# Attending: one PSUM bank for all key tiles in turns of four matmuls, and a longer rest in the gating

## The chip, the cores and the metric

The kernel runs on one core of one Trainium2 chip. The metric is the device time of one execution in microseconds (us). The kernel before takes 6137.45 us in the median of three runs (6137.38 to 6148.23).

## The reference

Input is x, 8 batches of 128 channels on a 36 x 36 grid, so 1296 tokens of 128 numbers per batch, all in float32. Cut to what matters:

```python
x = x + L0_conv_ref(group_norm(x), ...)         # convolutional attention block
t = tokens(x)                                   # (8, 1296, 128)
t = t + L1_attn_ref(layer_norm(t), ...)         # additive attention
t = t + L1_ffn_ref(layer_norm(t), ...)          # experts that choose their tokens

def L1_attn_ref(x, mask, Wq, bq, Wk, bk, w, bw):
    q, k = x @ Wq.T + bq, x @ Wk.T + bk
    scores = (tanh(q[:, :, None] + k[:, None]) * w).sum(-1) + bw
    return softmax(scores) @ x

def L1_ffn_ref(x, gate_w, gate_b, weight1, weight2):
    probs = softmax(x @ gate_w.T + gate_b, axis=tokens)   # 64 experts
    # each expert takes its 8 best tokens, pools them, runs two layers with a gelu,
    # and adds its output, weighted, to these tokens
```

The additive attention needs a tanh for every pair of tokens and every channel. Its scores are the bulk of the kernel's time.

## The kernel before

**Scores.** The kernel gets the scores from products of exponentials: for each pair of tokens it sums terms, and a term is a numerator divided by a denominator, where both are matmuls of a key feature (kf) with a query feature (qf). Queries of a batch are worked in three chunks of 432 (CH), keys in eleven tiles: ten of 128 and a last one of 16, which is put sixth (the list `order`, 0 to 4, 10, 5 to 9). One chunk and one key tile make a unit. A full unit has twelve slots, numbered k = 0 to 11, the small one has two. In all there are 2928 slots, and the loop of lines 1113 to 1146 writes out the program slot by slot.

In each slot, TensorE makes two numerators n and, for the slot three ahead (LAG), two denominators d (line 949). Each contracts 32 rows in two of three slots and 64 rows in the third. ScalarE takes the logarithm of d (line 972), and every second slot the exponential of its negative (line 975), which gives lq = 1/d. VectorE multiplies n by lq (line 1003), and GpSimd adds up the products (lines 1010 and 1012). In slots 2, 5, 8 and 11 (DVE_PAIRS) VectorE does the adding too (lines 992 to 999), so it has four operations there (three in slot 2) and not two.

**Banks.** The numerators and all side work share a pool of four PSUM banks, ps_n (line 151). A slot needs two of them for its n. `aux` takes one of the same four. The denominators have two double banks of their own.

**Side work.** All else of the layers is written as Python generators and taken up between the slots. They stand in four lanes, in this order of rank: first_of_all, urgent (the attending, and the first key features), gates (the gating) and background (the next batch's first layer, its tokens and key features). A generator yields what it wants next: `matmuls(rest)`, a turn on TensorE after so many slots, or `step(rest)`, a turn on the other engines. `TAKE` is a step in the next slot. `take_turns` (line 1072) runs the steps at the start of a slot, but not in DVE_PAIRS except for the first lane. `matmul_turn` (line 1077) runs one turn with matmuls at the end of a slot. Turns are paced: each turn's columns are counted (`bmm` adds the columns of its output, at least 128, and 20 more), every slot earns 400 (PACE), and a lane other than the first waits while the balance is below zero or the next slot is one of DVE_PAIRS. The gates lane also waits while urgent has work.

**Attending.** When the eleven exponentials e of a chunk are there (line 1032), `attend` (line 747) is put in the urgent lane. It works through the chunk's four query tiles of 108 tokens. For each, TensorE multiplies e by the normalized tokens xh, which carry a column of ones, so that the sum of the weights comes along: eleven products of 108 x 129 (function `weigh`). The product of the 16-token key tile uses xr, a copy of those tokens on the rows on which its e lies, and contracts 16 rows. The eleven are made in two turns of 6 and 5, each into a bank of its own. The first bank is copied to the tile `sums` (line 770), the second is added to it in the bank (line 772), and then VectorE closes the query tile: reciprocal (774), scaling and residual (775) and the statistics for the next normalization (779 and 780). For the last chunk of all, `attend_early` (line 724) sums nine key tiles while the scores of the last two are still being made.

**Gating.** `gate_logits` (line 793) follows for a whole batch. It computes the inverse root of the variances on GpSimd (`rsqrt`, into rs), and then for each chunk transposes the tokens (tp2), copies them (t2T), stores them, transposes them back in pairs (tp3), and scales each pair by rs (line 830). Between the copy and the first tp3 it asks for a rest of one slot (line 822). For the last batch it is called for one chunk at a time, from `attend`.

The order on every engine is the order of the written program. Semaphores between the engines are set by the framework.

Of the kernel before, what the change touches and what calls it, by code (L numbers as in the profile page):

```python
# [10 lines left out]
F32 = mybir.dt.float32  # L11
# [4 lines left out]
NB, C, H, W = 8, 128, 36, 36  # L16
# [7 lines left out]
T = 108  # L24
# [3 lines left out]
NKT = len(KT)  # L28
# [42 lines left out]
def kernel(  # L71
# [28 lines left out]
    nc = tc.nc  # L100
# [29 lines left out]
    with ExitStack() as loop, ExitStack() as score:  # L130
# [9 lines left out]
        chunks = pool("chunks", 8)  # L140
# [18 lines left out]
        def aux(name):  # L159
            return ps_n.tile([128, 512], F32, tag="n", name=name)  # L160
# [116 lines left out]
        def matmuls(rest=0):  # L277
            return (True, rest)
# [441 lines left out]
        def attend_early(b, c, es):  # L720

            xh, _, xr = prepared[b]
            held = [chunk_tile("sums") for _ in range(TPC // 2)]
            for i in range(TPC):
                at = (i % 2) * (C + 1)
                sums = early[i] = held[i // 2][:T, at : at + C + 1]
                for some in (order[:5], order[6 : NKT - 2] + order[5:6]):
                    pa = aux("pa1")[:T, : C + 1]
                    weigh(pa, i, some, es, xh, xr)
                    yield TAKE  # L730
                    if some[0] == order[0]:
                        nc.vector.tensor_copy(sums, pa)
                    else:
                        nc.vector.tensor_add(sums, pa, sums)
                    yield matmuls()

        def weigh(pa, i, some, es, xh, xr):

            for j in some:
                if j < NKT - 1:  # L740
                    e, v = es[j][:, i * T : (i + 1) * T], xh[:, j, :]
                else:
                    rows = slice(32 * i, 32 * i + REM)
                    e, v = es[j][rows, :T], xr[rows]
                bmm(pa, e, v, start=(j == some[0]), stop=(j == some[-1]))

        def attend(b, c, es):


            xh, _, xr = prepared[b]  # L750
            if c == 0:
                t2 = big_tile("t2").rearrange("p (t c) -> p t c", c=128)
                mv = two.tile([T, NT, 2], F32, tag="t2_mv", name="t2_mv")
                attended[b] = (t2, mv)
            t2, mv = attended[b]
            own = range(c * TPC, (c + 1) * TPC)
            for at in own:
                nc.sync.dma_start(t2[:T, at, :], tokd[b][at * T : (at + 1) * T])
            for i, at in enumerate(own):
                if i in early:  # L760
                    parts, sums = (order[NKT - 2 :],), early[i]
                else:
                    parts = (range(6), range(6, NKT))
                    sums = two.tile([T, C + 1], F32, tag="sums", name="sums")
                for some in parts:
                    pa = aux("pa1")[:T, : C + 1]
                    weigh(pa, i, some, es, xh, xr)
                    yield TAKE
                    if some[0] == 0:
                        nc.vector.tensor_copy(sums, pa)  # L770
                        yield matmuls()
                nc.vector.tensor_add(pa, pa, sums)
                inv = small.tile([T, 1], F32, tag="inv", name="inv")
                nc.vector.reciprocal(inv, pa[:, C : C + 1])
                nc.vector.scalar_tensor_tensor(
                    t2[:T, at, :], pa[:, :C], inv, t2[:T, at, :], ALU.mult, ALU.add
                )
                st = small.tile([T, 6], F32, tag="t2_st", name="t2_st")
                nc.vector.bn_stats(st, t2[:T, at, :])
                nc.vector.bn_aggr(mv[:, at, :], st)  # L780
                yield matmuls()
            if c == NCH - 1:
                prepared.pop(b)
            if b == NB - 1:
                yield from gate_logits(b, [c])
# [7 lines left out]
        def gate_logits(b, chunks):  # L793
# [23 lines left out]
            for c in chunks:  # L817
                tp, tt = turned(c, "t2T")
                yield TAKE
                nc.vector.tensor_copy(tt, tp[:, :CH])  # L820
                nc.sync.dma_start(t2d[b][:, c * CH : (c + 1) * CH], tt)
                yield matmuls(1)
                for j0 in range(0, TPC, 2):
                    tp = aux("tp3")
                    for j in (j0, j0 + 1):
                        turned_to(tp[:T, j * C : (j + 1) * C], tt[:, j * T : (j + 1) * T], ident)
                    yield TAKE
                    for j in (j0, j0 + 1):
                        t = c * TPC + j
                        nc.vector.tensor_scalar(  # L830
                            t2[:T, t, :], tp[:T, j * C : (j + 1) * C],
                            mv[:, t, 0:1], rs[:, t - tiles[0] : t - tiles[0] + 1],
                            ALU.subtract, ALU.mult,
                        )
                    yield matmuls()
# [522 lines left out]
```

The softmax here doesn't subtract the row's maximum and nothing guards it: scores larger than these inputs give would overflow.

## Time and profile before

| What | Value |
|---|---|
| Runs, median (lowest to highest) | 6137.45 us (6137.38 to 6148.23) |
| Profiled execution, its own time | 6140.74 us |
| Span of its instructions | 6139.0 us |
| Mean granted TensorE clock | 0.985 |
| TensorE busy / weight loads | 5957.9 us (97%) / 2862.1 us (47%) |
| ScalarE busy | 5279.9 us (86%) |
| VectorE busy | 4796.4 us (78%) |
| GpSimd busy | 4597.7 us (75%) |
| Attending's products of full key tiles (pa from xh and e) | 1920 records, 0.273 us in the median |
| Attending's products of the 16-token tile (pa from xr and e) | 192 records, 0.312 us in the median |
| Line 770, copy of the first sums | 92, 26.6 us busy |
| Line 772, addition of the two sums | 96, 28.0 us busy |

Times in the profile are microseconds unless marked ns. PE is TensorE, PEld its weight loads, DVE is VectorE, ACT ScalarE, POOL GpSimd, SP the engine that issues most DMAs. L949 is line 949 of the kernel. A float32 matmul leaves two records. An arrow in brackets names what ended the idle time of an engine before a row. The ends of matmuls are modelled and matmuls overlap, so that a busy TensorE is not one at its peak. A window is counted in us from the span's start.

### The profile page before, as it was taken

The numbers are of one execution on the slowest core, as the hardware profiler recorded it, in microseconds if no ns is written. First come the engines' busy times: TensorE is split into PE (matmuls) and PEld (weight loads), VectorE is DVE, ScalarE is ACT, GpSimd is POOL, SyncE is SP. The second block draws the span as 40 slices with busy tenths as digits, with TensorE's granted clock in tenths as the row PEclk, the third lists the DMA queues.
The fourth block names the chain that finished last, engine by engine and source line by source line (L and its number), as shares of the span: only waits on it lengthen the run. The fifth ranks groups of instructions, "written<-read, shape, count | busy, mean of one in ns | idle before, by whom it ended". The sixth has DMA issues, their size and how long they took to land.

```text
span 6139.0 us, 93072 instructions
## 1 busy us (share of the span) xinstructions
PE 5957.9 (97%) x33480; PEld 2862.1 (47%) x33480; DVE 4796.4 (78%) x9521; ACT 5279.9 (86%) x5371; POOL 4597.7 (75%) x2819
## 2 busy tenths in 40 slices
PE   7999999999999999999999999999999999999996
PEld 5454444544544445444455444454444544544443
DVE  4787878877788787877888777887778877788882
ACT  1888898888988888889998889888898888999990
POOL 4777777777787777778778786877777777787870
PEclk9999999999999999999999999999999999999997
DMA  1210011100110002100111001110011100110008
GB/s 44 70 37 22 25 62 38 34 25 28 68 43 20 26 27 71 39 24 23 44 55 39 22 24 59 44 39 22 20 65 40 34 25 28 58 50 29 28 20 297
DMA packets 151519, 270.87 MB, mean 44 GB/s; under 512 B 45648, under 2 KB 76752, under 8 KB 151056
## 3 DMA queue, kind: packets, MB, share of 16 engines
q1 hardware_dynamic: 151056, 264.92, 13.0%
q8 instruction: 264, 4.33, 0.3%
q14 instruction: 199, 1.63, 0.1%
HBM read 200.41 MB, written 64.19 MB: 43 GB/s over the span
## 4 chain that ended last, share of the span: by engine, by line
PE 77%; ACT 7%; DVE 6%; issue 6%; POOL 2%; DMA 1%; SPq 0%; DVEq 0%; POOLq 0%; ACTq 0%
PE n L949 37%; PE d L949 12%; PE pa L284 7%; PE pc L284 5%; ACT lq L972 5%; PE s L284 3%; PE pk L284 3%; PE pq L284 3%; DVE rp L1003 2%; DVE n L997 1%; DVE accd L999 1%; PE d L954 1%; ACT lq L975 1%; DMA w<-in_weight_dram 1%; PE n L954 1%
## 5 line engine op out<-in xcount | busy, mean ns | idle before, releaser
L1012 POOL TENSOR_TENSOR accp<-accp,rp 128x864 f32<-128x864 f32 x1440 | 2915.8, 2025 | 1041.0 <-DVE rp L1003 948.8
L949 PE MATMUL n<-qf,kf 32*128 32x432 f32 (+1 forms) x11520 | 3325.3, 574 | 46.5 <-ACT e L1032 13.3
L949 PE MATMUL d<-qf,kf 32*128 32x432 f32 (+1 forms) x11520 | 2991.6, 561 | 38.7 <-ACT lq L972 38.2
L972 ACT ACTIVATE lq<-d 128x864 f32<-128x864 f32 x2928 | 2524.2, 878 | 542.6 <-PE d L949 512.1
L1003 DVE TENSOR_TENSOR rp<-n,lq 128x432 f32<-128x432 f32 x3912 | 2173.3, 600 | 743.5 <-PE d L949 542.8
L975 ACT ACTIVATE lq<-lq 128x1728 f32<-128x1728 f32 (+1 forms) x1464 | 2398.2, 1638 | 46.3
L949 PEld LDWEIGHTS n<-qf,kf 32*128 32x128 f32 (+1 forms) x11520 | 1206.4, 184 | 1600.3 <-DVE rp L1003 581.5
L949 PEld LDWEIGHTS d<-qf,kf 32*128 32x128 f32 (+1 forms) x11520 | 1090.0, 185 | 422.1 <-issue 224.7
L997 DVE TENSOR_TENSOR n<-n,lq 128x432 f32<-128x432 f32 x1440 | 814.9, 608 | 142.1 <-PE n L949 88.5
L999 DVE TENSOR_TENSOR accd<-n,accd 128x432 f32<-128x432 f32 x1440 | 866.3, 602 | 24.6
L1010 POOL TENSOR_TENSOR accp<-rp 128x864 f32<-128x864 f32 x240 | 485.2, 2022 | 197.7 <-DVE rp L1003 195.6
L711 POOL TENSOR_SCALAR qf<-qf,cs_s 128x432 f32<-128x432 f32 x192 | 260.9, 1365 | 45.0 <-ACT qf L710 44.4
L284 PEld LDWEIGHTS pa<-xh,e 128*108 128x108 f32 x1920 | 222.5, 174 | 131.1 <-DVE rp L1003 56.0
L1021 POOL TENSOR_TENSOR accd<-accp,accd 128x432 f32<-128x432 f32 x240 | 265.2, 1105 | 18.8
L1019 POOL TENSOR_TENSOR accp<-accp 128x432 f32<-128x432 f32 x240 | 264.4, 1102 | 16.7
L284 PE MATMUL pa<-xh,e 128*108 128x129 f32 x1920 | 262.9, 283 | 8.7 <-ACT e L1032 5.2
L284 PE MATMUL s<-q,k 128*116 128x432 f32 x480 | 230.3, 568 | 1.7 <-DVE q L316 1.4
L284 PEld LDWEIGHTS pk<-xT,a_k 128*128 128x128 f32 x1408 | 171.2, 192 | 107.0 <-DVE n L997 33.7
L462 POOL TENSOR_TENSOR tot<-tot,e 116x432 f32<-116x432 f32 x192 | 212.0, 1104 | 6.0 <-ACT e L471 4.6
L471 ACT ACTIVATE e<-s 116x432 f32<-116x432 f32 x240 | 124.9, 520 | 98.3 <-PE s L284 97.9
L284 PE MATMUL pa<-e,vw 116*128 116x432 f32 x480 | 204.6, 549 | 0.0
L284 PE MATMUL pk<-xT,a_k 128*128 128x128 f32 (+1 forms) x1408 | 202.5, 287 | 0.1
(213 smaller groups left out, 3788.4 us busy)
## 6 DMA issues: line engine op xcount, KB each, us to landing
kf<-kd SPq DMA_DIRECT2D x239, 512.0 KB
kd<-ks SPq DMA_DIRECT2D x158, 256.0 KB
w<-in_weight_dram SPq DMA_DIRECT2D x32, 1024.0 KB
wk_t<-wk_t_d SPq DMA_DIRECT2D x7, 768.0 KB
wv_t<-wv_t_d SPq DMA_DIRECT2D x7, 768.0 KB
wq_t<-wq_t_d SPq DMA_DIRECT2D x7, 768.0 KB
x<-in_x_dram SPq DMA_DIRECT2D x8, 648.0 KB
t<-tokd SPq DMA_DIRECT2D x96, 54.0 KB
```

Source lines behind the costliest of these rows:

```text
L284: mm(out, lhsT, rhs, **kw)
L711: nc.gpsimd.tensor_scalar(qf[:, 1, :], qf[:, 0, :], cs_s[:, q : q + 1], None, ALU.mult)
L949: mm(outs[h][:, :CH], kf[rows[h], q, :], qf_of[b, c, q][rows[h], part, :], start=True, stop=True)
L972: nc.scalar.activation(lq[:, o : o + n, :], d[:, :n, :CH], AF.Ln)
L975: nc.scalar.activation(some, some, AF.Exp, scale=-1.0)
L997: mult(ns[h], ns[h], lq[:, o + h, :])
L999: nc.vector.tensor_add(live["d"], ns[h], live["d"])
L1003: mult(rp[:, h, :], n, lq[:, o + h, :])
L1010: nc.gpsimd.tensor_add(live["p"], live["r"], rp)
L1012: nc.gpsimd.tensor_add(live["p"], live["p"], rp)
L1019: nc.gpsimd.tensor_add(s[:, 0, :], s[:, 0, :], s[:, 1, :])
L1021: nc.gpsimd.tensor_add(d, s[:, 0, :], d)
```

## The change

Three things change.

The eleven products of a query tile all go into one bank, in the order of `order`, and `weigh` becomes a generator: it gives up its turn after every fourth product. So a query tile takes three turns, of 4, 4 and 3 products, and the product of the 16-token tile is the sixth. The copy to `sums` and the addition fall away, except for the four query tiles of the last chunk, whose early sums are added as before.

In `attend_early` the nine products of a query tile go into one bank in turns of 4, 4 and 1. One addition per query tile falls away.

In `gate_logits` the first chunk asks for a rest of four slots, not one, between the copy of t2T and the first tp3, except in the last batch.

```diff
         def attend_early(b, c, es):
...
                 sums = early[i] = held[i // 2][:T, at : at + C + 1]
-                for some in (order[:5], order[6 : NKT - 2] + order[5:6]):
-                    pa = aux("pa1")[:T, : C + 1]
-                    weigh(pa, i, some, es, xh, xr)
-                    yield TAKE
-                    if some[0] == order[0]:
-                        nc.vector.tensor_copy(sums, pa)
-                    else:
-                        nc.vector.tensor_add(sums, pa, sums)
-                    yield matmuls()
+                pa = aux("pa1")[:T, : C + 1]
+                yield from weigh(pa, i, order[: NKT - 2], es, xh, xr)
+                nc.vector.tensor_copy(sums, pa)
+                yield matmuls()
 
         def weigh(pa, i, some, es, xh, xr):
-            for j in some:
+            for x, j in enumerate(some):
                 if j < NKT - 1:
                     e, v = es[j][:, i * T : (i + 1) * T], xh[:, j, :]
                 else:
                     rows = slice(32 * i, 32 * i + REM)
                     e, v = es[j][rows, :T], xr[rows]
-                bmm(pa, e, v, start=(j == some[0]), stop=(j == some[-1]))
+                last = x == len(some) - 1
+                bmm(pa, e, v, start=(x == 0), stop=last)
+                if last:
+                    yield TAKE
+                elif x % 4 == 3:
+                    yield matmuls()
 
         def attend(b, c, es):
...
             for i, at in enumerate(own):
+                pa = aux("pa1")[:T, : C + 1]
+                yield from weigh(pa, i, order[NKT - 2 :] if i in early else order, es, xh, xr)
                 if i in early:
-                    parts, sums = (order[NKT - 2 :],), early[i]
-                else:
-                    parts = (range(6), range(6, NKT))
-                    sums = two.tile([T, C + 1], F32, tag="sums", name="sums")
-                for some in parts:
-                    pa = aux("pa1")[:T, : C + 1]
-                    weigh(pa, i, some, es, xh, xr)
-                    yield TAKE
-                    if some[0] == 0:
-                        nc.vector.tensor_copy(sums, pa)
-                        yield matmuls()
-                nc.vector.tensor_add(pa, pa, sums)
+                    nc.vector.tensor_add(pa, pa, early[i])
                 inv = small.tile([T, 1], F32, tag="inv", name="inv")
...
         def gate_logits(b, chunks):
...
                 nc.sync.dma_start(t2d[b][:, c * CH : (c + 1) * CH], tt)
-                yield matmuls(1)
+                yield matmuls(1 if c > chunks[0] or b == NB - 1 else 4)
```

## The prediction

> **What bounds the kernel now.** I began with the page: its engine shares and the chain that ended last.
>
> ```profile
> span 6139.0 us, 93072 instructions
> ...
> PE 5957.9 (97%) x33480; PEld 2862.1 (47%) x33480; DVE 4796.4 (78%) x9521; ACT 5279.9 (86%) x5371; POOL 4597.7 (75%) x2819
> ...
> PE 77%; ACT 7%; DVE 6%; issue 6%; POOL 2%; DMA 1%; SPq 0%; DVEq 0%; POOLq 0%; ACTq 0%
> ```
>
> TensorE (PE) carries 77% of the chain, but that is an average over stages. So I took two stretches of the last batch, where no other background work stands: one without side work, and one that is the attending of one chunk (slots 6 to 23 after it became due).
>
> ```profile
> core 0: us, PE busy (x) PEld busy (x) DVE busy (x) ACT busy (x) POOL busy (x), PEclk, DMA share, GB/s
> 5516.00:5549.00 33.00, 32.24 (x156) 12.69 (x154) 25.45 (x47) 32.61 (x36) 30.02 (x18) 1.00 0.05 17
> 5564.90:5600.50 35.60, 35.48 (x234) 20.52 (x232) 31.23 (x74) 30.08 (x30) 24.41 (x14) 1.00 0.08 26
> ```
>
> Without side work ScalarE (ACT) is busy 32.61 of 33 us and sets the pace. While attending it idles 5.5 us of 35.60: there TensorE and VectorE (DVE) hand the path to each other, as the timeline of the first attended query tile shows.
>
> ```profile
> 5564.41 1.58 PE L284 MATMUL pa<-xh,e 128*108 128x129 f32 x12 [0.54 <-DVE accd L999]
> 5564.91 1.11 DVE L1003 TENSOR_TENSOR rp<-n,lq 128x432 f32<-128x432 f32 x2
> ...
> 5565.92 0.63 PE L949 MATMUL n<-qf,kf 32*128 32x432 f32 x2
> ...
> 5566.86 0.99 PE L949 MATMUL n<-qf,kf 64*128 64x432 f32 x4
> 5567.02 1.12 DVE L1003 TENSOR_TENSOR rp<-n,lq 128x432 f32<-128x432 f32 x2 [0.69 <-PE d L949]
> ...
> 5568.06 1.12 DVE L997 TENSOR_TENSOR n<-n,lq 128x432 f32<-128x432 f32 x2
> 5568.51 1.13 PE L284 MATMUL pa<-xh,e 128*108 128x129 f32 x8
> 5569.57 0.36 PE L284 MATMUL pa<-xr,e 16*108 16x129 f32 x1
> ...
> 5570.24 0.29 DVE L772 TENSOR_TENSOR pa<-pa,sums 108x129 f32<-108x129 f32 x1
> ...
> 5571.58 1.10 DVE L1003 TENSOR_TENSOR rp<-n,lq 128x432 f32<-128x432 f32 x2
> ```
>
> Read from it: a turn of six products (12 records, two per product) holds TensorE 5565.92-5564.41 = 1.51 us; eight full records up to the 16-row ones take 1.06. So 0.11 per record and 0.19 per turn: 1.07 for four products, 0.85 for three. A slot of 32-row products takes TensorE 5566.86-5565.92 = 0.94, one of 64-row products 5568.51-5566.86 = 1.65. Products reach VectorE 5567.02-5565.92 = 1.10 after they begin. Slot 8 is VectorE's: 3.52 us from 5568.06 to 5571.58, 2.26 of its own four operations and 1.26 of the query tile's closing (lines 772 to 780). Slot 7 was TensorE's: VectorE idled 0.69.
>
> The gating's wait is in the answer on its scale column t_rs, here as it stands for the whole kernel:
>
> ```profile
>   POOL t_rs L265: 6.6, 7
> ```
>
> That is 0.94 us each in seven batches.
>
> **What the skill says.** The Trainium skill, "TensorEngine Tiling (Array Packing)", Key Properties: changing the tiling mode drains TensorE. The trace agrees in part: weights for a full-array turn are loaded only after 0.62 us of idle behind row-tiled products, and each turn costs its fixed 0.19. "TensorE: Matmul & The Clock Gate", The mechanism: a weight load overlaps running products only if its rows differ. Here the 16-row products at 5569.57 overlap the next slot's (n also begins at 5569.58), so at the end of a turn they cost nothing. "Perfetto Trace Analysis", Optimization Strategy: repeated equal gaps can mean too little PSUM for the next tile; the trace has TensorE's weight loads for n waiting 581.5 us on VectorE's line 1003 over the kernel.
>
> **The change, part by part.** The build of the changed kernel (not run) gives the order and PSUM banks of both programs. In both, 23 of 24 attendings lie in the loop. Before, each has eight turns of 6 and 5 products, 16 of them in slots 6, 8, 9, 11, 14, 15, 17, 20. After, all 23 have twelve, of 4, 4, 3, in slots 6, 8, 9, 11, 12, 14, 15, 17, 18, 20, 21, 23.
>
> Removed: 92 copies (0.289 us each, line 770), 92 of the 96 additions of line 772 (0.292; the four early query tiles keep theirs) and the early part's four (line 734, 0.285): 188 operations, 26.6+26.9+1.1 = 54.6 us of VectorE. The copies overlap TensorE's next products; only the addition of 0.30, in the closing, lies on the path where VectorE has it: the closing falls from 1.26 to 0.95.
>
> Added on TensorE, per query tile: one turn, 0.19; and the 16-row product, formerly last, now sixth, amid full ones. Its switch into row mode was shared with the turn's end; now it stands alone, and so does one back. The trace does not show it inside a turn. Lower bound 0 if loads hide it, upper 0.4 (two whole fixed turn costs); I take 0.20, one switch more.
>
> Added waits: one of four banks (ps_n) stays with the query tile over three turns. By the bank numbers, in every slot meanwhile the second product pair waits for the first VectorE result of the slot before (0.56 plus 0.10 for the signal; in a 64-row slot's successor 1.65 plus 0.10). Behind it TensorE, in order, holds that slot's second n product, its d products for ScalarE three slots on, and the next turn.
>
> Now the path, with slot 6's VectorE start at 0 and the turn at -0.50. Four products end at 0.56; the second n of slot 7 waits until 0.66; VectorE starts 7 at 1.66 (before 2.11). TensorE is free at 1.60, but slot 8's second n waits for slot 7's first result, 1.66+0.66 = 2.32, so the next turn starts at 2.32+1.65 = 3.97 instead of 3.25. VectorE has 8 at 1.66+1.04 = 2.70. The second turn with the 16-row product takes 1.27, to 5.24; 9 starts at 6.34 (before 6.67), a third turn runs from 6.18 to 7.03, and the closing ends at 7.45+0.95 = 8.40: 10 starts at 8.41 (before 8.49). Going on likewise: slot 12 at 11.84 (13.06), 15 at 18.78 (18.49), 18 at 25.47 (25.09), 21 at 30.97 (31.25), 24 at 37.91 (35.55). The same rules give before's starts within 0.1 for slots 7 to 15. The gain at the closings is lost to the held bank in 64-row slots, and three more slots contain a turn: +2.35 us per attending, 23 times 54.0.
>
> Against this: in batches 0 to 6 the last turns push other background turns out of slots 21 and 23. With two of those there, slots 6 to 24 take 36.82 instead of 35.55, or 0.64 each; the same work comes later, and I let half of it land where ScalarE hides it: 14 chunks x 0.64 = -9.0.
>
> The gating: in seven batches its first tp3 turn moves from slot 26 to 32, and everything of it behind, the stores of t2T and of the gates on SP's queue included. It ends VectorE's 0.94 waits: -6.6 at most, nothing at least (if ScalarE sets the pace by then); I take -6.6. The delay costs nothing: the stores are needed only in the last stage, and the key load behind them was issued two key tiles (some 48 us) ahead. The next batch's layer 0 waits for the gates, but by the order its work in chunks 1 and 2 begins at the same slots again. Without that cover one turn would cost its 0.64.
>
> The tail: one more product and the last query tiles' third turn, +1.
>
> Sum on the profiled execution: 54.0-9.0-6.6+1 = +39, span 6139 to 6178. That execution took 6140.74, the runs 6137.38 to 6148.23; on the median of 6137.45 this is 6176, 0.6% slower.
>
> **Rivals.** VectorE decides (faster): the closing at slot 8 really is VectorE's, and 54.6 us leave it. If in two of four query tiles both removed operations, 0.58, come off the path and the bank wait is hidden in VectorE's own 2.18 of a pair slot: 23 x 1.16 + 6.6 = -33, or 6104. It takes over if the twelve turns' waits in 64-row slots, about 0.7 each, fall below those savings. Against it: 2 of 8 turns only show VectorE on the chain there, TensorE is busy 35.48 of 35.60.
>
> The sides cancel: no switch cost (0.2 four times, of which some 0.6 on the path, -14) and the displaced turns all hidden (-9 more), the bank waits half as long (some 1.7 us of them per attending lie on the path by the worked starts, so 23 x 0.85 = -20): 39-43 = -4, or 6133, in a span of 6125 to 6149.
>
> The switch costs more: at 0.4, the four of a chunk add 0.8 more, and slots 9, 13, 18, 22 are TensorE's: 23 x 0.8 = 18; with no background hidden (+9) and no gating gain (+7), 6210.
>
> That the change does not do what it says is excluded by the built order.
>
> **Numbers.** Forecast slower by some 40: 0.56; dearer switch: 0.17; cancel: 0.14; VectorE decides: 0.13. The runs tell about 0.2%, 12 us, from nothing. So faster 0.13, same 0.14, slower 0.73. The range reaches down into the VectorE case, with its end at 6120, and up past the dear one to 6222; the forecast's own range is 6155 to 6200.
>
> **What would show it.** In the attend stretch of the last batch, slots 6 to 24 in 37 to 39 us rather than 35.55; four closings of 0.95 without line 772's addition for full tiles; waits of n on VectorE up, most in 64-row slots; records after a 16-row product starting 0.2 late; no wait of the gating on t_rs. I am wrong if that stretch is shorter than 35.5, or if the stretch fits but stages without pa turns change by over 10 us.

## The result and the profile after

The changed kernel takes 6210.02 us in the median of four runs (6204.94 to 6213.82), the kernel before 6137.43 beside it (6137.38 to 6148.23). That is 1.0113 of the time before, with a 95% interval of 1.0096 to 1.0131: slower by 1.1%, or 73 us. The forecast was 6176, its range 6120 to 6222. The sign was right and the range held the time, but the loss is nearly twice the forecast one, and the time lies outside the 6155 to 6200 that the forecast gave for its own account. The time 6210 is that of the rival with the dearer switch. It is shown below that this rival has its switch right, and its total only by chance.

The page of the kernel after, its head and the shares of the chain that ended last:

```profile
span 6209.3 us, 92949 instructions
...
PE 6012.2 (97%) x33480; PEld 2854.4 (46%) x33480; DVE 4760.1 (77%) x9333; ACT 5279.3 (85%) x5371; POOL 4597.7 (74%) x2819
...
PE 80%; ACT 6%; issue 5%; DVE 4%; POOL 2%; DMA 1%; SPq 0%; DVEq 0%; POOLq 0%; ACTq 0%
```

VectorE lost 4796.4 - 4760.1 = 36.3 us of work and falls from 6% to 4% of the chain. TensorE rises from 77% to 80%, with the same number of matmuls. In the shares of the chain, that is what changed.

To see where, take for every slot the start of VectorE's first operation in it, in both traces, and compare the stretches. (In the file after, lines from about 770 on have numbers that are lower by 8: n and d are line 941, rp is 995.) The spans differ by 70.3 us:

| Where | After less before, us | Forecast, us |
|---|---|---|
| slots 6 to 24 of the 23 chunks with an attending | +60.4 | +36.0 |
| all other slots, batches 0 to 6 | -13.1 | +2.4 |
| all other slots, batch 7 | +12.8 | 0 |
| after the loop | +10.3 | +1 |
| ahead of the loop | -0.2 | 0 |

The forecast is laid out by place here. Its -9.0 for the turns that are pushed out is -18 in slots 6 to 24 and +9 in the slots that take them, so that 54.0 - 18 = 36.0 stands in the first row and 9.0 - 6.6 = 2.4 in the second.

The windows of the kernel after that answer to those of before. The first is the stretch without side work, the second the attending of the last batch's chunk 1, slots 6 to 24. The last two lie in slots 29 to 32 of the same chunk and are read further down. Columns: window, its length, busy time of each engine with its number of instructions, granted TensorE clock, DMA.

```profile
core 0: us, PE busy (x) PEld busy (x) DVE busy (x) ACT busy (x) POOL busy (x), PEclk, DMA share, GB/s
5558.23:5591.23 33.00, 32.25 (x156) 12.71 (x154) 25.46 (x47) 32.61 (x36) 30.28 (x18) 1.00 0.05 17
5607.16:5645.67 38.51, 38.51 (x235) 20.81 (x236) 29.62 (x65) 30.11 (x30) 26.41 (x15) 1.00 0.09 28
...
5655.00:5660.00 5.00, 3.35 (x15) 1.12 (x14) 2.80 (x8) 3.40 (x4) 2.24 (x2) 0.78 0.00 0
5660.00:5664.60 4.60, 4.60 (x16) 1.53 (x16) 2.84 (x7) 0.89 (x1) 1.59 (x1) 0.50 0.00 0
```

Without side work nothing moved: ScalarE is again busy 32.61 of 33 us. The attending takes 38.51 us where it took 35.55, and TensorE is busy in all of it. VectorE has 1.6 us less to do there than before and gets nothing for it.

The timeline of the first query tile of that attending, in the kernel after:

```profile
5606.65 1.14 PE L284 MATMUL pa<-xh,e 128*108 128x129 f32 x8 [0.54 <-DVE accd L991]
5607.16 1.11 DVE L995 TENSOR_TENSOR rp<-n,lq 128x432 f32<-128x432 f32 x2
...
5607.72 0.71 PE L941 MATMUL n<-qf,kf 32*128 32x432 f32 x2
...
5609.48 0.18 PEld L941 LDWEIGHTS n<-qf,kf 64*128 64x128 f32 x1 [0.44 <-DVE rp L995]
...
5611.12 0.47 PE L284 MATMUL pa<-xh,e 128*108 128x129 f32 x2
...
5611.52 0.47 PE L284 MATMUL pa<-xr,e 16*108 16x129 f32 x2
...
5611.92 0.69 PE L284 MATMUL pa<-xh,e 128*108 128x129 f32 x4
...
5612.54 0.63 PE L941 MATMUL n<-qf,kf 32*128 32x432 f32 x2
...
5613.48 0.91 PE L284 MATMUL pa<-xh,e 128*108 128x129 f32 x6
...
5614.87 0.35 DVE L767 SCALAR_TENSOR_TENSOR t<-pa,inv,t 108x128 f32<-108x128 f32 x1
```

Three turns are seen, of 8, 8 and 6 records (a float32 product leaves two). The turn with the 16-row product takes 5612.54 - 5611.12 = 1.42 us, where a turn of four full products takes 5607.72 - 5606.65 = 1.07. The 0.44 at 5609.48 is the second pair of numerators of a 64-row slot waiting for VectorE. The prediction expected this wait from the bank that is held, and the same slot of the kernel before has no such gap. Before the closing there is no addition of line 772 any more.

The forecast's slot starts can be laid beside the measured ones, in us from slot 6's:

| Slot | 7 | 8 | 9 | 10 | 12 | 15 | 18 | 21 | 24 |
|---|---|---|---|---|---|---|---|---|---|
| before, measured | 2.10 | 3.14 | 6.66 | 8.48 | 13.06 | 18.48 | 25.08 | 31.24 | 35.55 |
| after, worked out | 1.66 | 2.70 | 6.34 | 8.41 | 11.84 | 18.78 | 25.47 | 30.97 | 37.91 |
| after, measured | 1.66 | 2.70 | 6.48 | 8.53 | 12.01 | 18.98 | 25.80 | 31.31 | 38.51 |

Last, two lines of the view of waits (engine, line, what it waited for, us in total, times, longest), of the kernel after:

```profile
POOL t_rs L265 <- DVE ve L260: 29.2, 1, 29.2
...
DVE t L767 <- DMA t<-tokd: 22.0, 1, 22.0
```

The gating's seven waits of VectorE on t_rs are gone. There is one wait of 22 us on a DMA now, which the kernel before does not have, and t_rs itself is once kept waiting for 29.2.

### The profile page after: what moved, and what is told of

Same layout as the page of the kernel before. It is cut to its first block, busy times and chain, and to the rows that moved or that the text cites. A ratio compares the mean times of both kernels' runs of the same rounds, so it can differ in the third digit from the quotient of the medians.

```text
span 6209.3 us, 92949 instructions
## 1 busy us (share of the span) xinstructions
PE 6012.2 (97%) x33480; PEld 2854.4 (46%) x33480; DVE 4760.1 (77%) x9333; ACT 5279.3 (85%) x5371; POOL 4597.7 (74%) x2819
## 4 chain that ended last, share of the span: by engine, by line
PE 80%; ACT 6%; issue 5%; DVE 4%; POOL 2%; DMA 1%; SPq 0%; DVEq 0%; POOLq 0%; ACTq 0%
PE n L941 40%; PE d L941 11%; PE pa L284 8%; PE pc L284 5%; ACT lq L964 4%; PE s L284 3%; PE pk L284 3%; PE pq L284 3%; DVE rp L995 2%; DVE n L989 1%; PE d L946 1%; PE n L946 1%; DMA w<-in_weight_dram 1%; POOL accp L1004 1%; DVE accd L991 1%
## 5 line engine op out<-in xcount | busy, mean ns | idle before, releaser
L941 PE MATMUL d<-qf,kf 32*128 32x432 f32 (+1 forms) x11520 | 3023.3, 562 | 44.7 <-ACT lq L964 43.6
L995 DVE TENSOR_TENSOR rp<-n,lq 128x432 f32<-128x432 f32 x3912 | 2181.5, 601 | 860.7 <-PE d L941 666.8
L941 PEld LDWEIGHTS n<-qf,kf 32*128 32x128 f32 (+1 forms) x11520 | 1190.1, 184 | 1588.0 <-DVE rp L995 546.2
L991 DVE TENSOR_TENSOR accd<-n,accd 128x432 f32<-128x432 f32 x1440 | 868.3, 603 | 24.7
L284 PE MATMUL pa<-xh,e 128*108 128x129 f32 x1920 | 310.3, 292 | 8.2 <-ACT e L1024 4.1
```

The lines of the kernel that those rows point to most:

```text
L284: mm(out, lhsT, rhs, **kw)
L941: mm(outs[h][:, :CH], kf[rows[h], q, :], qf_of[b, c, q][rows[h], part, :], start=True, stop=True)
L991: nc.vector.tensor_add(live["d"], ns[h], live["d"])
L995: mult(rp[:, h, :], n, lq[:, o + h, :])
```

## The experiments

### The 16-row product at the end of its turn

```diff
-                yield from weigh(pa, i, order[NKT - 2 :] if i in early else order, es, xh, xr)
+                yield from weigh(pa, i, order[NKT - 2 :] if i in early else range(NKT), es, xh, xr)
```

> The changed kernel with the product of the 16-token key tile last in its query tile, not sixth; turns of 4, 4 and 3 in one bank stay. Theory (held bank, extra turn, and a mode switch of 0.2 us in the middle of the turns): slots 6 to 24 of an attending fall from 38.5 to about 37.8 us, 23 x 0.7 = 16 us in all, 6194. Rival (the switch costs nothing in the middle of a turn): 6210. Rival (the switch is the main cost, 0.4 or more): 6180 or less.

Measured: 6177.22 us (6173.17 to 6179.24), 1.0058 of the kernel before (1.0042 to 1.0075), so 33 us less than the kernel after. That is twice what the theory gave; the rival in which the switch is the main cost is nearer. The same attending, windows view and timeline of this kernel:

```profile
5573.31:5610.44 37.13, 37.13 (x235) 20.69 (x236) 29.69 (x64) 30.25 (x30) 26.51 (x15) 1.00 0.09 28
```

```profile
5577.27 1.14 PE L284 MATMUL pa<-xh,e 128*108 128x129 f32 x8
...
5578.34 0.63 PE L941 MATMUL n<-qf,kf 32*128 32x432 f32 x2
...
5579.28 0.69 PE L284 MATMUL pa<-xh,e 128*108 128x129 f32 x4
...
5579.90 0.47 PE L284 MATMUL pa<-xr,e 16*108 16x129 f32 x2
...
5580.10 0.62 PE L941 MATMUL n<-qf,kf 32*128 32x432 f32 x1
```

The second turn, now of four full products, takes 5578.34 - 5577.27 = 1.07 us again, and the turn that ends with the 16-row product holds TensorE for 0.82. In the middle of full products the 16-row product costs 1.42 - 1.07 = 0.35 us more than a full one, at the end nothing more (the turn of three full ones was worked out at 0.85). The attending falls from 38.51 to 37.13, or 1.38, about four times 0.35: all four are on the path. Over all 23 attendings slots 6 to 24 are 60.4 - 30.7 = 29.7 us shorter, 1.29 each.

### One bank, in the old turns of six and five

```diff
-                yield from weigh(pa, i, order[NKT - 2 :] if i in early else order, es, xh, xr)
+                yield from weigh(pa, i, order[NKT - 2 :] if i in early else range(NKT), es, xh, xr)
-                elif x % 4 == 3:
+                elif x % 6 == 5:
```

> The changed kernel with the 16-token product last and turns of 6 and 5 products, still all in one bank and without the copy and the addition. Against the kernel before only the held bank is new (and the longer rest in the gating), and 188 VectorE operations are gone. Worked as in the prediction: slots 6 to 24 at about 35.0 us against 35.55 before, since the held bank costs about 0.7 twice and the shorter closing and the turns give 1.9 back; with the gating, 6115 to 6135. Rival (the held bank is the main cost): slots 6 to 24 at 36.5 or more, 6155 to 6180.

Measured: 6216.30 us (6205.27 to 6235.96), 1.0125 (1.0105 to 1.0144). A turn less for each query tile, and no faster than the kernel after. The theory's total fell, and the rival's 6155 to 6180 with it. In the last batch's chunk 1 the attending takes 36.11 us, 0.56 more than before where something less than before was thought possible, and the tail is as short as before (153.5 us against 152.2). But the loop outside the attend stretches is 46 us longer than before, spread over all middle batches. There the turns of the other lanes stand in other slots. The next two experiments take the gating's rest by itself.

### The gating's rest back to one

```diff
-                yield matmuls(1 if c > chunks[0] or b == NB - 1 else 4)
+                yield matmuls(1)
```

> The changed kernel with the gating's rest of one slot as before. Theory (the longer rest ends seven waits of 0.94 us): 6 us slower than the changed kernel, 6216, and the waits on the scale column are back at 6.6 us. Rival (the rest pushes other turns into dearer slots): up to 10 us faster than the changed kernel.

Measured: 6246.88 us (6245.67 to 6247.56), 1.0171 (1.0155 to 1.0186). The rest of four is worth 37 us in the kernel after, not 7. Seven waits of 0.94 us don't explain this, and they are not even back: VectorE waits for t_rs in no place of this trace. The longer attending alone moves the gating far enough to end them.

### The rest of four alone, in the kernel before

```diff
-                yield matmuls(1)
+                yield matmuls(1 if c > chunks[0] or b == NB - 1 else 4)
```

> The kernel before with one edit: the rest of four slots in the gating's first chunk of seven batches. Its attending is that of before; from the gating on, its background turns stand in the same slots as those of six_five_xr_last. Theory of the displaced turns: the rest moves every later background turn of the batch, and it is these new places that cost (the loop outside the attend stretches was 43 us longer in six_five_xr_last): 35 to 55 us longer than before, 6172 to 6192. Rival (the prediction's step): only the seven waits of 0.94 us on t_rs go, 0 to 7 us shorter, 6130 to 6137.

Measured: 6192.67 us (6187.44 to 6199.52), 1.0085 (1.0070 to 1.0100): 52 us longer than the kernel before, at the upper end of what the theory of displaced turns gave. The same edit loses 52 us with the old turns and wins 37 with the new ones. In the written order, the first two tp3 turns stand in slots 26 and 27 before, in 32 and 33 after, and in the long kernels (this one and the two ahead) in 29 and 30. All turns behind them differ too. The rest is not a local edit.

### One bank alone, every other turn where it was

The kernel before with one bank in turns of six and five and the rest of one.

```diff
-                elif x % 4 == 3:
+                elif x % 6 == 5:
...
-                yield matmuls(1 if c > chunks[0] or b == NB - 1 else 4)
+                yield matmuls(1)
```

> The kernel before with the other half alone: one bank for all key tiles in the old turns of six and five, the 16-row product last, rest of one. Every turn of the whole program stands in the slot that it has before. Theory (the held bank costs what the undisturbed chunk showed, 0.57 us for an attending): 23 x 0.57 = 13 us longer than before, 6150, all of it in slots 6 to 24 of the chunks. Rival A (the prediction's step: VectorE's relief is worth more than the bank that is held): shorter than before. Rival B (the held bank costs more where other turns stand beside it, as the 28 us of six_five_xr_last over all its attend stretches say): 6165.

(The diff is against the kernel after with the 16-row product last.) Measured: 6153.97 us (6149.24 to 6157.65), 1.0022 (1.0013 to 1.0031): 13 us longer than before, as the theory had it. 15.6 us of the difference of the traces lie in slots 6 to 24, all other slots together differ by 0.6. Those 0.6 are a sum of +4.4 in batch 0, +5.2 in batch 7 and -8.9 between them, though every turn has its old slot: so much can differ between two executions with one order. Rivals A and B fall.

### The addition kept

```diff
                 if i in early:
                     nc.vector.tensor_add(pa, pa, early[i])
+                else:
+                    nc.vector.tensor_add(pa, pa, zeros[:T])
```

> one_bank_alone with one more edit: in the closing of each full query tile VectorE adds a tile of zeros to the bank, an addition of the same shape as that of the two sums, so that the closing is as long as before while the bank is held over both turns. The result does not change. It measures what VectorE's relief in the closing is worth. Theory (the prediction's step: the addition of 0.29 us is on the path where the closing stands in a slot in which VectorE has the path, two of the four): 23 x 0.6 = 14 us longer than one_bank_alone, 6168. Rival A (all four closings on the path): 23 x 1.17 = 27 us, 6181. Rival B (the relief is hidden): within 4 us of one_bank_alone.

(`zeros` is a tile of zeros.) Measured: 6180.70 us (6179.17 to 6183.06), 1.0074 (1.0060 to 1.0088). With spans of 6179.8 and 6155.1 that is 24.7 us more than one bank alone. It lies nearer to Rival A's 27 than to the theory's 14. In slots 6 to 24 it is 21.3 us, 0.93 for each attending, which is three of the four additions of 0.29. The window of the same attending, first with the addition, then without it:

```profile
5599.39:5636.43 37.04, 36.88 (x234) 20.83 (x232) 30.71 (x69) 30.11 (x30) 24.32 (x14) 1.00 0.08 22
```

```profile
5575.70:5611.87 36.17, 36.14 (x234) 20.84 (x232) 29.74 (x66) 29.67 (x30) 24.34 (x14) 1.00 0.07 23
```

With this the attending can be taken apart, in the same chunk each time: 35.55 before; 37.04 with the bank held, the copies gone and the addition kept (+1.49); 36.17 without the addition (-0.87); 37.13 with a third turn (+0.96); 38.51 with the 16-row product in the middle (+1.38). The 1.49 is what the held bank costs and the absent copies save, together. In this stretch the loads of weights for n wait 2.8 us for VectorE's rp before and 4.4 with the addition kept, as a held bank would have it. The kernel paid for the removed addition with the held bank already, and the other two came on top.

### The loads of t ahead of the weights

In the kernel after, the attending of the last chunk is still behind its early part when the loop ends. There the program takes one more step of the urgent lane, then issues nine loads of 1 MB of the last stage's weights, and then runs the rest of the lane. Before, that one step loads t. After, it only ends the early part, and the second part, whose first act is to load t, comes behind the nine loads. Timeline of the kernel after (SPq is the queue of DMA issues):

```profile
6046.58 1.75 SPq L1170 DMA_DIRECT2D w<-in_weight_dram  x3
...
6065.82 5.18 SPq L759 DMA_DIRECT2D t<-tokd  x4
...
6075.34 0.35 DVE L767 SCALAR_TENSOR_TENSOR t<-pa,inv,t 108x128 f32<-108x128 f32 x1 [21.95 <-DMA t<-tokd]
```

```diff
         urgent.run(len(slots))
+        urgent.run(len(slots))
         for _ in range(9):
             load_next()
```

> The changed kernel with one more step of the last attending's generator before the nine weight loads of the last stage, so that its four token loads stand ahead of them on the queue, as they did before. Theory (the last query tiles wait 22 us for these loads behind nine transfers of 1 MB, part of which the last stage gets back because it waits for weights): 8 to 12 us faster than the changed kernel, about 6200, and the wait before line 767 gone. Rival (the last stage is set by its weights anyway): no difference, 6210.

Measured: 6199.13 us (6193.14 to 6202.31), 1.0092 (1.0077 to 1.0107), 11 us less than the kernel after. The stretch after the loop falls from 162.6 to 152.9 us, to within a microsecond of the kernel before, and the closing waits for nothing:

```profile
6045.23 0.35 DVE L767 SCALAR_TENSOR_TENSOR t<-pa,inv,t 108x128 f32<-108x128 f32 x1
```

A wait of 22 us had cost 10. Most of the rest vanished in the last stage's own waits: from the end of the loop on, its matmuls of line 1249 (1248 in the kernel after) wait 17.1 us for weights here, and 9.0 in the kernel after.

### The last batch's logits in the gating's lane

```diff
-            if b == NB - 1:
+            if b == NB - 1 and c < NCH - 1:
+                gates.append(gate_logits(b, [c]))
+            elif b == NB - 1:
```

> The kernel after with one edit: in the last batch the logits of chunks 0 and 1 go to the gating's own lane and not the urgent one, so that they are not run all at once in slot 30. Theory (in the last batch the longer attending runs into the next chunk's second key tile, where what is left of the urgent lane is put out in one slot): slots 24 to 36 of chunks 1 and 2 get back 4.8 and 3.4 us, 6 to 8 us shorter than after, 6202 to 6204. Rival (the same work costs the same wherever it stands): within 2 us of after.

Measured: 6200.38 us (6199.51 to 6202.73), 1.0097 (1.0082 to 1.0112), span 6199.0: 10.3 us shorter than the kernel after. Slots 24 to 36 of chunks 1 and 2 give back 5.1 and 3.7 us. The two windows at the end of the first table of windows tell what had happened: in slot 30 all that is left of the urgent lane is written out at once, a tp3 turn, a tp2 turn and the logits, and each waits for what VectorE makes of the one ahead. TensorE is busy 3.35 of 5 us. Then its granted clock falls, to 0.78 in the mean of this window and to 0.50 in the next. What follows at half clock is ordinary score work.

### The three mended together

> The kernel after with three edits together: 16-row product last, both urgent generators ended ahead of the nine weight loads, logits of the last batch in the gating's lane. Theory (three separate costs that add up): 32.8 + 10.9 + 7 = 51 us shorter than after, 6159 (6150 to 6168). What then stands against the kernel before is the third turn, 23 x 1.0 = 23 us, and the held bank. Rival (they overlap, since one cost hides another): above 6170.

Measured: 6156.23 us (6150.96 to 6161.47), 1.0024 (1.0015 to 1.0034). The edits of the 16-row product, of the loads and of the logits add up: 54 us against 51 expected. With these three mended the kernel takes as long as one bank alone in turns of six and five (6153.97), and still longer than the kernel before.

### What a turn costs depends on its place

The rest of four also moves the turns of the key features. Before, the last two of them stand in slots 0 and 2 of the next batch's first chunk. In rest_four_alone the whole sequence of them begins earlier, in slots 82 and 83, and ends inside the last chunk. Windows of the kernel before: slots 24 to 36 of the first chunk of batches 3 and 2, which the next experiment needs, slots 74 to 86 of batch 3's last chunk, and slots 0 to 6 of batch 4.

```profile
2428.41:2455.68 27.27, 25.66 (x114) 10.98 (x113) 22.81 (x48) 20.27 (x19) 20.99 (x13) 0.81 0.10 32
1692.44:1716.12 23.68, 22.13 (x114) 10.82 (x113) 22.22 (x48) 20.12 (x19) 19.40 (x11) 1.00 0.12 36
3023.26:3043.39 20.13, 19.84 (x117) 9.87 (x117) 18.57 (x37) 19.88 (x20) 16.04 (x9) 1.00 0.09 31
3120.59:3131.74 11.15, 11.06 (x68) 5.56 (x69) 8.39 (x16) 9.89 (x11) 10.64 (x11) 1.00 0.24 62
```

The last two stretches in rest_four_alone:

```profile
3039.80:3062.28 22.48, 22.44 (x132) 12.38 (x131) 18.35 (x36) 21.71 (x23) 18.05 (x11) 1.00 0.18 59
3139.30:3150.05 10.75, 9.52 (x52) 4.19 (x47) 8.11 (x15) 10.55 (x11) 10.52 (x9) 1.00 0.13 31
```

Slots 74 to 86 take 22.48 - 20.13 = 2.35 us more: ScalarE had set the pace there, busy 19.88 of 20.13, and now TensorE is busy 22.44 of 22.48 and ScalarE 21.71. In slots 0 to 6 the absence of two turns wins 0.40, since ScalarE fills 10.55 of the 10.75 that are left.

These are not the same two turns. Two timelines of the kernel before, of TensorE and of ScalarE, show a turn of a full key tile and one of the 16-token tile, which comes last:

```profile
3118.41 1.16 PE L284 MATMUL pk<-xT,a_k 128*128 128x128 f32 x8
3120.43 1.06 PE L284 MATMUL pk<-xT,a_k 128*128 128x16 f32 x8
...
3119.82 0.60 ACT L687 ACTIVATE ks<-pk 128x512 f32<-128x512 f32 x1
3123.09 0.20 ACT L687 ACTIVATE ks<-pk 128x64 f32<-128x64 f32 x1
```

The two that come into slots 82 and 83 are full ones, the two that leave slots 0 and 2 are small: nearly the same for TensorE, a third for ScalarE. So 2.35 against 0.40 is in part a matter of size. That place counts too is seen in slots 110 to 122 of the last chunk, where the two small ones take the places of two full ones: there the time falls by only 0.18 us in the mean of six batches.

To test it, the turns were put back into their old slots:

```diff
         def keys(b, tiles):
...
-            yield matmuls(1)
+            yield matmuls(4 if b > 1 else 1)
```

> rest_four_alone with one more edit: from the third batch on, the first turn of the next batch's key features rests four slots and not one. By the written order this moves two turns of each of six batches, from slots 82 and 83 of the last chunk to slots 0 and 2 of the next batch's first chunk, where the kernels before and after have them; every other turn stays where rest_four_alone has it. Theory (a turn costs what its place allows: slots 74 to 86 go at ScalarE's pace and the two turns push TensorE beyond it, while slots 0 to 6 hold them for 0.39 us): 2.35 - 0.39 = 1.96 us less in each of six batches, 12 us shorter than rest_four_alone, 6181. Rival (a turn costs its TensorE time wherever it stands): no change beyond 3 us.

Measured: 6191.13 us (6181.16 to 6203.07), 1.0092 (1.0078 to 1.0105). In total no gain that can be told. In the places concerned it did much as expected, a little smaller: slots 74 to 86 are 1.69 us shorter in each of the six batches (10.1 in all), slots 0 to 6 are 0.39 longer in five of them (3.8 in all). So 1.69 of the 2.35 belong to the two turns; the other 0.66 belong to the turns of the tokens, which still stand three slots earlier. Of the 6.3 us won, 5.5 are lost again in other slots and 3.0 after the loop, and 3.2 are won ahead of the loop, where the two programs are the same. But for slots 110 to 122 the turns stand as in rest_four_alone there, and the granted clock is not the same: the trace's record of it has 143 us at 0.50 in the loop up to slot 119 of the last chunk, against 109 in rest_four_alone. The theory's numbers hold near these slots and not for the sum.

A second try at the same, meant to beat both kernels, took the kernel before, the rest of four and a rest of seven ahead of the key features.

> The kernel before with the rest of four in the gating and, from the third batch on, a rest of seven ahead of the first turn of the next batch's key features. By the written order, chunks 1 and 2 of the middle batches then have the turns of before, the first chunk has from slot 24 on those of after, and four more key feature turns move from slots 85 to 89 to slots 3, 5, 23 and 24 of the next batch's first chunk. Attending is that of before. Theory (places decide: slots 74 to 98 give back some 4 us in each of six batches, slots 0 to 24 take some 2, and the first chunk's slots 24 on cost nothing or gain 2): 10 to 20 us shorter than the kernel before, 6118 to 6128. Rival (the turns in slots 0 to 24 push the attending, and cost what they save): 6135 to 6150.

Measured: 6156.25 us (6155.09 to 6160.77), 1.0035 (1.0021 to 1.0049). The theory's 6118 to 6128 fell, and the rival's 6135 to 6150 with it. The middle batches 2 to 6 came out even (+1.8 us together): each won 2.7 in slots 74 to 98 of the last chunk and lost 3.1 in the first chunk. Batch 1, in which the order is that of rest_four_alone, lost 10, batch 7 lost 7.

### The clock behind a wait

The first two windows of the kernel before above have the same turns, the same matmuls and the same gating in them. One takes 27.27 us and the other 23.68. The difference is the granted clock, 0.81 and 1.00. In both the same wait stands ahead of it, here that of batch 3 in the timeline of the kernel before:

```profile
2431.80 2.30 POOL L265 TENSOR_TENSOR t_rs<-ve,neg_half 108x12 f32<-108x12 f32 x1
...
2434.13 0.73 DVE L830 TENSOR_SCALAR t<-tp,t_mv,t_rs 108x128 f32<-108x128 f32 x2 [0.88 <-POOL t_rs L265]
...
2434.91 2.11 PE L949 MATMUL n<-qf,kf 32*128 32x432 f32 x3 [1.17 <-DVE t L830]
```

VectorE waits 0.88 us for t_rs, TensorE, for want of a bank, 1.17 us behind it. Right after that, from 2435.85 on, the record shows 6.83 us at 0.50. The Trainium skill, "TensorE: Matmul & The Clock Gate", section "What's actually happening", says that the clock has two settings, full and half, and is set by TensorE's activity in windows of some 3.4 us. The trace agrees: all intervals are at 0.50 and 3.41, 6.83 or 10.24 us long but for some in the last stage. The page puts the fall after an idle window; here TensorE was busy 2.07 of the 3.41 us ahead, and the clock still fell.

The same wait of TensorE, 1.17 to 1.19 us, stands in batches 1, 2, 3 and 6. Right behind it the clock falls in batches 1 and 3 and not in 2 and 6. In the record of the loop every change of the clock lies on one grid of 3.41 us. These are the grid's windows of the kernel before that the wait falls into, for batches 1, 2, 3 and 6:

```profile
957.89:961.30 3.41, 2.06 (x13) 0.77 (x12) 2.48 (x6) 3.00 (x3) 3.41 (x2) 1.00 0.02 5
1695.17:1698.58 3.41, 2.43 (x16) 0.72 (x12) 2.49 (x6) 3.10 (x4) 3.41 (x3) 1.00 0.11 38
2432.44:2435.85 3.41, 2.07 (x12) 0.48 (x5) 2.50 (x7) 2.71 (x3) 3.41 (x2) 1.00 0.00 0
4644.28:4647.69 3.41, 2.22 (x15) 0.72 (x12) 2.50 (x6) 3.10 (x4) 3.41 (x3) 1.00 0.06 20
```

In batches 1 and 3 the whole wait lies inside one window, with TensorE busy 2.06 and 2.07 us, and the next window is at half clock. In batches 2 and 6 it runs over a window's end, so that TensorE is busy 2.43 and 2.22 us, and the clock stays. Batches 5 and 7 go with 1 and 3 (2.06 and 2.08), batch 4 with 2 and 6 (2.71; its fall comes one window later). So whether this wait is followed by half clock depends on where it lies on the grid. It is no full rule: in this trace one fall follows a window of 2.66 us, that of batch 4 one of 2.73, and one window of 1.83 is followed by none.

The last experiment fills such gaps in the kernel before, with two products behind the gating's second tp3 turn and four in slot 41 of the last chunk, where TensorE waits 2.97 us for a tanh on ScalarE:

```diff
+                    if c == chunks[0] and j0 > 0 and b < NB - 1:
+                        for _ in range(2):
+                            mm(tp[:, :256], ident, tt[:, :256], start=True, stop=True)
...
-            yield matmuls(2)
+            yield matmuls(1)
+            warm = aux("warm")
+            for _ in range(4):
+                mm(warm[:, :256], ident, r[:, :256], start=True, stop=True)
+            yield matmuls(1)
```

> The kernel before with products of no use put where TensorE stands idle and its granted clock then falls to 0.50 for 3.4 or 6.8 us: two of 256 columns behind the second tp3 turn of the first chunk's gating (slot 27, where TensorE waits 1.17 us behind t_rs), and four in slot 41 of the last chunk (where it waits 2.97 us for ScalarE's tanh of the next batch's first layer). They go into columns that nobody reads; the result is the same, and every other turn stays in its slot. Theory (what a wait costs TensorE is mostly the half clock behind it, and full windows prevent that): the intervals at 0.50 in slots 24 to 48 of chunks 0 and 2 go, 34 and 44 us of them in batches 1 to 7, of which half is time: 20 to 38 us shorter than the kernel before, 6100 to 6117; the waits themselves stay. Rival A (the half clock falls into time that ScalarE sets anyway): within 5 us of before. Rival B (the added products delay the next slot): 5 to 20 us longer.

Measured: 6123.03 us (6119.62 to 6131.61), 0.9975 of the kernel before (0.9968 to 0.9982), 16 us faster than it. It beats both kernels. Of the same two stretches, batches 3 and 2, its windows say:

```profile
2420.86:2444.55 23.69, 23.00 (x119) 11.41 (x117) 22.23 (x47) 20.11 (x19) 19.66 (x11) 1.00 0.12 37
1686.68:1710.35 23.67, 23.00 (x118) 11.40 (x117) 22.22 (x47) 20.11 (x19) 19.38 (x11) 1.00 0.12 35
```

Both take the same time now. The wait on t_rs is still there (7.2 us in all), and where the clock had not fallen before (batch 2 here) the added products cost nothing. No interval at half clock is left in slots 24 to 48 of chunks 0 and 2 of batches 1 to 7. These slots are 18.7 us shorter over all batches. By the record it is 72 us at half clock that went (the 44 of the expectation should have been 38). They were worth a quarter of their length, not the half that was expected. That the rest had fallen into time that ScalarE or VectorE sets is likely, and was not shown.

## Why the prediction was right and wrong

**The bound, and the sign.** Right. TensorE and VectorE hand the path over, and the relief for VectorE is outweighed by what is added on TensorE's side. Relief alone is worth 0.87 us per attending by the addition that was kept, near the 1.16 of the rival in which VectorE decides; that rival falls because the held bank, with the copies gone, costs 1.49, more than all of the relief. The span was to grow by 39 us and grew by 70: of the 31 us that were missed, 22 are the tail and the last batch, and 9 the attending with the displaced turns and the gating.

**The attend stretch, +2.35.** Measured +2.96 in the undisturbed chunks, inside the 37 to 39 us that were named. The worked slot starts hit slots 7 and 8 exactly and miss slot 9 by 0.14. This is the term that was mis-sized here: the 16-row product's switch was taken at 0.20 and costs 0.35, four times per attending, which makes the 0.6. The upper bound of 0.4, two whole fixed turn costs, was the better value: two changes of mode stand alone in the middle of the turn, in and back, and 0.20 paid for one. The Trainium skill, "TensorEngine Tiling (Array Packing)", section "Key Properties", says that a change of mode drains TensorE, which fits, and gives no price. That the product costs nothing more at the end of a turn was right. The premise named for it, that a weight load overlaps running products only of other rows, is not what the trace shows: in the turn at 5606.65 the full-array loads are 0.17 us long and begin 0.11 apart, while full-array products of 0.27 run (by their modelled ends). The other two terms were near: the third turns at four times 0.19 for a measured 0.96, the held bank at some 1.7 for a measured 1.49.

**Waits of n on VectorE up.** Wrong for the whole change. In the attend stretch of the last batch the waits of TensorE's weight loads for n on VectorE's rp are 2.8 us before and 2.1 after, over the kernel 581.5 and 546.2. With the bank held alone they do go up, to 4.2; the longer turns then hide them. The cost of those turns shows in the opposite wait, of VectorE for the denominators (through ScalarE's lq): 2.2 before and 7.4 after in the stretch, 542.8 and 666.8 over the kernel.

**Displaced turns, -9.0, and the gating, -6.6.** Their account is wrong, though the sum with the attending is not far off: +60.4 - 13.1 = +47.3 in the table's first two rows against 54.0 - 9.0 - 6.6 = +38.4. By place the forecast misses both, by 24 up and 15 down, and that these partly cancel is chance. Turns were pushed out in the second chunks as forecast, where the stretch of batches 1 to 6 grew by only 1.68; in the third chunks it grew by some 3.06, no less than where nothing is pushed out. The gating's -6.6 was put down to the rest, but the waits on t_rs are gone with a rest of one as well. And the delay was costed as nothing because chunks 1 and 2 begin at the same slots again. By the order they do, but the slots between are filled anew, and this is what the rest was worth: without it, 37 us more. With the old turns it costs 52. The step looked at what the rest ends, one wait in a batch, and not at the order that the rest sets for every lane behind it. The wait was mis-sized too: 0.94 us of VectorE was said to be the most it can be worth, but a wait that starves TensorE can be followed by some microseconds at half clock, which was 3.6 us in batch 3 and nothing in batch 2.

**The tail, +1.** Wrong, +10.3. The step counted matmuls and one turn more, and missed a DMA: with three turns the early part isn't done when the loop ends, and the loads of t go behind 9 MB of weights on SP's queue. For the gating the forecast had followed the stores on SP's queue; here it did not follow the loads.

**The last batch, 0.** Missed. In the last batch the attending is followed by its logits in the same lane, and three more slots per attending push them into the place where the rest of the lane is written out at once. It costs 10 us by the run that takes them out of the lane, half clock included.

**The rivals.** The dearer switch came true as a mechanism (0.35 of 0.4), at 23 x 1.3 = 30 us for all of it. But its 6210 also took 9 us for background that isn't hidden and 7 for a gating that wins nothing, and it had only 1 us for the tail and the last batch, which make 23 of the measured 70. That the totals meet is chance.

**What stays open.** Why turns in slots 29 and 30 make a bad order and those in 26 and 27, or 32 and 33, a good one was followed to single places (two turns of the key features, 1.69 us in slots 74 to 86; the clock behind a wait) but not summed up to the 52 and 37 us. Why the other slots of batches 0 to 6 won 13.1 us in the kernel after is open with it. Which gaps make the clock fall is settled for the one wait on t_rs, by its place on the grid, and not as a rule.

## What to carry to other kernels

A change that frees an engine can be paid by what it holds longer: ask for each removed operation which buffer now lives longer and whose next instruction waits for it. When work takes more turns in a shared queue, follow it to the places where the queue has a deadline or is emptied by force, such as the end of a loop, the last iteration or a load that must be issued first; here these corners cost 20 of 73 us. And do not cost a shift in the order of background work by the one wait that it ends; run it alone, in both orders.

## What was not expected of the hardware

A product of 16 rows between products of the full array costs 0.35 us more than one of 128 rows, and nothing more when row-tiled work follows it.

A wait of TensorE of some 1.2 us can be followed by 3.4 to 6.8 us at half its clock, although TensorE was busy 2.07 of the 3.41 us ahead. The same 12 slots then take 27.27 us, not 23.68. The same wait a little later on the grid of 3.41 us, with TensorE busy 2.22 or 2.43, left the clock as it was. Six products that compute nothing, put into such gaps in each batch, made the kernel before 0.25% faster (0.18% to 0.32%).
